# Four graph layers on one core: one return transfer per group of attention, x in memory as it lies on the chip, and layer 0's last outputs inside layer 1's first steps

## The chip, the cores and the metric

The kernel runs on one core of one Trainium2 chip. TensorE (PE) multiplies matrices; VectorE (DVE), ScalarE (ACT) and GpSimd (POOL) work elementwise; SyncE (SP) issues most transfers and POOL issues the rest. Each engine takes its instructions in the order of the program and waits on semaphores for the others. The metric is the device time of one execution in microseconds. Times are medians of several runs; one execution is profiled, and its trace is what the document reads.

## The reference

The input x has shape (128, 64, 256): 128 graphs of 64 nodes with 256 features, that is 8192 tokens. Four layers follow each other, each as x = x + layer(max(layernorm(x), 0)), all in float32:

```
layer 0: h = relu(adj @ (x @ Wg0 + bg0)); h = relu(adj @ (h @ Wg1 + bg1))
         for p in 1..4: cut the nodes into windows of p, run an LSTM over each window,
                        put its last hidden state in the place of the window's last node
layer 1: Xq = H @ W_lin.T; Xv = H @ W_val.T                    (4 heads, 512 edges)
         e = a . leaky_relu(Xq[src] + Xq[dst]) + log(adj[src, dst] + eps)
         attn = softmax of e over the edges with the same src
         Y[src] += attn * Xv[dst]; result Y @ W_out.T
layer 2: agg = A_hat @ x; batchnorm(relu(batchnorm(agg @ W1.T + b1)) @ W2.T + b2)
layer 3: attention of every node over the nodes that adj allows (one head)
```

## The kernel before

The 8192 tokens are cut into NCH = 16 chunks of CHUNK = 512; four chunks make a group (NGR = 4 groups of 2048). A chunk is on the chip as a tile [128, 4, 256]: partition p holds four tokens, tile i holds tokens 128 i to 128 i + 127. Between layers, x is kept in memory in one tensor per chunk, `xa[n]` after layer 0 and `xb[n]` after layer 1, in the order of tokens: 512 rows of 1 KB. The values of layer 1, `xv_mem[n]`, are stored as [128, 4, 256] instead.

Instructions are issued by a framework that orders them by its own priorities; `late(...)` holds an instruction at its place in the program's order. It also inserts the waits between engines and the waits for memory that is used again.

**Layer 0.** Graph convolutions of the 16 chunks run first. `edge_tables()` is a generator, stepped between them, that prepares small tables for layer 1 on DVE, among them `row_of`: for each of the 512 edges (NE = 4 columns of 128) the row of the `field` in which its attention goes. The fields are cleared at the same time by transfers on SP. Then come the LSTMs, for w = 1 to 4 steps and in two halves (groups 0 and 1, groups 2 and 3). PE's products are at L643; the elementwise gates follow in a pipeline, slot by slot, and a gate's tail runs two slots after its products. `group_out(g, c)` (L768) closes a group: for two chunks it transposes the hidden state back (`add_transposed`: four transposes on PE, L167, into one bank; then an add on DVE, L172, to the tile `xres`), and stores `xa[n]` from POOL (L776). The original x for that add is loaded by `fetch_x` (L764) into one of four `xres` buffers. When the last group's LSTM ends, two calls of `group_out` are left, for chunks 12, 14, 13 and 15; they run at the end of layer 0, after the last gate. Chunks 0 and 1 are loaded and normed for layer 1 during the last LSTM (`first_norms1`).

**Layer 1.** It opens with the transposes of chunk 0 (`transpose_features`, L153; copied to `hTs[0]` by ACT, L156) and `project(0)`, `project(1)` (L948). Then `edges(q)` runs for q = 0 to 31, two tiles of 128 tokens each: `gather` (PE L964, copied by ACT L970, leaky ReLU on DVE L971), `project` of the two tiles after next, in even steps the transposes of the next chunk, in odd ones the scaling of the chunk after it, and `score` (L980). `load_x1` (L875) brings a chunk's x from `xa` to one of two buffers. The weights of layer 2 (`w1T` and so on) are loaded on SP ahead of the loads of x.

After each group of eight steps `edge_softmax(g)` is stepped in between later work. It ends by scattering the attention of the group into DRAM: POOL issues eight indirect transfers (L1074), four for each parity par (even and odd graphs lie in the lower and the upper 64 partitions), to `fields1[2 * g + par]`. A field has T * T rows of 64 values, one row for each pair of nodes, and E more rows for edges whose pair has come up already. From the field the attention comes back to the chip as `dense[g]` [128, 64, 64] (L1054): for groups 0 to 2 one transfer of 1 MB for each parity, each as soon as its parity's four scatters have landed; for the last group four of 0.5 MB. `turn_attention(n)` (L1130, half on ACT and half on DVE) puts a chunk's share into `att`.

From step 24 on, `values_of(n)` finishes chunk after chunk: `weigh` (PE L1148: attention times values), `put_out` (PE L1169: times W_out; DVE L1179: add x), `sums` (statistics for layer 2, on DVE and POOL), a store of `xb[n]`. `fetch(n)` loads, two chunks ahead, the values `xv_in` (L1111) and x (`xo`, L1121) on SP. Layers 2 and 3 load x from `xb`.

Of the kernel before, what the change touches and what calls it, by code (L numbers as in the profile page):

```python
# [30 lines left out]
def gnn_stack_kernel(ctx: ExitStack, tc: tile.TileContext, a: dict, out: bass.AP):  # L31
# [21 lines left out]
    xa = [dram.tile([CHUNK, D], F32, tag=f"xa{n}", name=f"xa{n}") for n in range(NCH)]  # L53
    xv_mem = [dram.tile([P, 4, D], F32, tag=f"xv{n}", name=f"xv{n}") for n in range(NCH)]
    xb = [dram.tile([CHUNK, D], F32, tag=f"xb{n}", name=f"xb{n}") for n in range(NCH)]
# [203 lines left out]
    row_of = tabs.tile([P, NE], I32, tag="row_of", name="row_of")  # L259


    FIELD = T * T + E
    NF = 2 * NGR
# [4 lines left out]
    def edge_tables():  # L268
        with ExitStack() as setup:
# [99 lines left out]

            nc.vector.tensor_scalar(earlier, earlier, 0.0, None, ALU.is_equal)  # L370
            nc.vector.tensor_scalar(index, index, float(T * T), None, ALU.add)
# [3 lines left out]
            nc.vector.tensor_copy(row_of, pair)  # L375
# [31 lines left out]

    with ExitStack() as l0:
        w0 = l0.enter_context(tc.tile_pool(name="w0", bufs=1))
# [175 lines left out]
        xres = lpool("xres", 4)  # L585
# [176 lines left out]
        def fetch_x(n):  # L762
            xt = xres.tile([P, 4, D], F32, tag="xres", name="xres")
            nc.sync.dma_start(out=xt, in_=token_tiles(a["x"], n))  # L764
            return xt
# [3 lines left out]
        def group_out(g, c):  # L769

            for u in range(2):
                n = 4 * g + 2 * u + c
                xt = residual.pop(n)
                for ip in range(2):
                    add_transposed(xt, 2 * ip, hTs0[g % 2][:, u], c * CHUNK + ip * 256)
                nc.gpsimd.dma_start(out=token_tiles(xa[n]), in_=xt)  # L776
                if g < 2:
                    m = n + NCH // 2
                    nc.sync.dma_start(
                        out=hTs0[g][:, u, :, c * CHUNK : (c + 1) * CHUNK], in_=hmem[m]  # L780
                    )
# [28 lines left out]
        for slot in range(len(tasks) + 2):  # L810
            new = tasks[slot] if slot < len(tasks) else None
            if new:
                step = steps[new[0]]
                one = step.gate(new[1])
                next(one)
# [11 lines left out]
            if new:  # L827
                next(one)
                flight.append((new, one))
                at, k = new[0], new[2]  # L830
                while outs and outs[0][0] <= slot:
                    group_out(*outs.pop(0)[1:])

                new_half = at + 1 < len(steps) and at and steps[at + 1].w == 1 < step.w
                if k == len(step.gates) - (1 if new_half else 2) and at + 1 < len(steps):
                    steps[at + 1].prepare()
                if step.w == MAX_SKIP and step.t == 2 and k < 2:
                    for u in range(2):
                        n = 4 * step.g + 2 * u + k
                        later.append((slot, "x", n))  # L840
# [7 lines left out]
            if old:  # L848
                (at, q, k), step = old[0], steps[old[0][0]]
                if k == len(step.gates) - 1:  # L850
                    if at + 1 == len(steps) or steps[at + 1].phase != step.phase:
                        phase_over(step.phase)
                    if step.phase == len(phases) - 1 and step.t == 1 and step.g == NGR - 1:

                        t_ = wsp.tile([P, 2, 4, 2, P], F32, tag="wih", name="x_first", bufs=2)
                        flat = t_.rearrange("p k q j m -> p k (q j m)")
                        norms1 = {}
                        for n in range(2):
                            xt = flat[:, n, :].rearrange("p (i d) -> p i d", i=4)
                            nc.sync.dma_start(out=xt, in_=token_tiles(xa[n]))  # L860
                            norms1[n] = Norm(xt)
                        norm_steps = first_norms1(norms1)
                    if step.w == MAX_SKIP and step.t == MAX_SKIP - 1:
                        outs += [(slot + 1, step.g, 0), (slot + 2, step.g, 1)]
        for _ in norm_steps:
            pass
        for _, g, c in outs:
            group_out(g, c)
    psums["banks"] = None
    w12 = ctx.enter_context(tc.tile_pool(name="w12", bufs=1, side="right"))  # L870
    xin1 = l01.enter_context(tc.tile_pool(name="xin1", bufs=2, side="right"))

    def load_x1(n, chunks=xa):
        xt = xin1.tile([P, 4, D], F32, tag="xin1", name="xin1")
        nc.sync.dma_start(out=xt, in_=token_tiles(chunks[n]))  # L875
        return xt


    with ExitStack() as l1:
# [7 lines left out]

        t1 = pool("t1", 2)
        lrp = pool("lrp", 6)
        t3 = pool("t3", 4)  # L890
        w1 = pool("w1", 1)
        vp = pool("vp", 3)
        KEPT = 4
        vk = pool("vk", KEPT)
        yp = pool("yp", 2)
        xo = pool("xo", 4)
        e1 = pool("e1", 1)
        attp = pool("attp", 3)
        attc = pool("attc", 3)
# [4 lines left out]
        nc.sync.dma_start(out=wout, in_=a["W_outT"])  # L904


        w1T = w12.tile([P, 2, 512], F32, tag="w1T", name="w1T")
        nc.sync.dma_start(out=w1T, in_=a["W1T"])
        w2T = w12.tile([P, 4, D], F32, tag="w2T", name="w2T")
        nc.sync.dma_start(out=w2T, in_=a["W2T"])  # L910
        w1S = w12.tile([P, 3, 2, P], F32, tag="w1S", name="w1S")
        w1Q = quarter_sums(w1T.rearrange("p k (q j m) -> p k q j m", q=2, j=2), w1S)
        x_rs = w12.tile([P, NCH, 4], F32, tag="x_rs", name="x_rs")
        x_nm = w12.tile([P, NCH, 4], F32, tag="x_nm", name="x_nm")
        vec = {}
        for name, width in (("b1", 4), ("g1", 4), ("be1", 4), ("b2", 2), ("g2", 2), ("be2", 2)):
            vec[name] = w12.tile([P, width], F32, tag=name, name=name)
            nc.sync.dma_start(out=vec[name], in_=a[name])
        hTs, queries, values, scores, waiting = {}, {}, {}, {}, []
# [20 lines left out]
        def project(it):  # L940

            n, i = it // 4, it % 4
            if i == 0:
                kept = n >= NCH - KEPT
                values[n] = (vk if kept else vp).tile([P, 4, D], F32, tag="xv", name="xv")
# [44 lines left out]
        def edge_softmax(g):  # L990
# [52 lines left out]
            sent = [[], []]  # L1043

            dense[g] = attp.tile([P, T, T], F32, tag="dense", name="dense")

            def bring_back(par, parts=1):
                for k in range(parts):
                    part_back(par, k, parts)

            def part_back(par, k, parts):

                r, s = slice(par * T, (par + 1) * T), slice(k * 32 // parts, (k + 1) * 32 // parts)
                back = nc.gpsimd.dma_start(  # L1054
                    out=dense[g][r, :, :].rearrange("p (o s) r -> p o s r", o=2)[:, :, s, :],
                    in_=fields1[2 * g + par][: T * T, :].rearrange("(t o s) r -> t o s r", t=T, o=2)[
                        :, :, s, :
                    ],
                )
                if g == NGR - 1:  # L1060
                    late(back)
                for ins in sent[par]:
                    tc.add_manual_dep(
                        back.ins,
                        ins.ins.name,
                        mybir.DependencyInfo(mybir.DependencyClass.Sync, mybir.DependencyReason.DATA),
                        reason="rows of the field",
                    )

            if g == NGR - 1:  # L1070
                yield
            for par in range(2):
                for ec in range(NE):
                    ins = nc.gpsimd.indirect_dma_start(  # L1074
                        out=fields1[2 * g + par][:, :],
                        out_offset=bass.IndirectOffsetOnAxis(ap=row_of[:, ec : ec + 1], axis=0),
# [3 lines left out]
                    for earlier in sent[par]:  # L1080
                        tc.declare_no_dep(ins.ins, earlier.ins, reason="different rows")
                    sent[par].append(ins)
                    if g == NGR - 1:
# [7 lines left out]
                        if len(sent[0]) + len(sent[1]) in (3, 6):  # L1091
                            yield
                    elif ec % 2:
                        yield
            if g == NGR - 1:

                for k in range(2):
                    for par in range(2):
                        part_back(par, k, 2)
            else:  # L1100
                bring_back(0)
                yield
                bring_back(1)

        def fetch(n):
# [6 lines left out]
            if n < NCH - 3:  # L1112
                xt = xo.tile([P, 4, D], F32, tag="xo", name="xo")
# [7 lines left out]
            nc.sync.dma_start(out=xt, in_=token_tiles(xa[n]))  # L1121
            fetched[n] = (xv, xt)

        def turn_attention(n):

            g, m = n // 4, n % 4
            att = attc.tile([P, 2, 8, T], F32, tag="att", name="att")
# [55 lines left out]
        def sums(n, xt, keep=False):  # L1183
# [6 lines left out]
            rs, nm = x_rs[:, n, :], x_nm[:, n, :]  # L1190
# [51 lines left out]
        def flush_stores():  # L1242
            while stores:
                m, xt = stores.pop()
                nc.sync.dma_start(out=token_tiles(xb[m]), in_=xt)
# [11 lines left out]
        def edges(q):  # L1257
# [5 lines left out]
            for it in tiles:  # L1263
                if it + 2 < NT:
                    project(it + 2)
            if not odd:
# [20 lines left out]
        hTs[0] = t1.tile([P, 2, CHUNK], F32, tag="hT1", name="hT1")  # L1287
        for ip in range(2):
            transpose_features(norms1[0].h, hTs[0], ip)
# [3 lines left out]
        for q in range(NT // 2):  # L1293
            edges(q)
            last_one = q == NT // 2 - 1
# [10 lines left out]
        def scale_x(n, xt, keep=late):  # L1306

            h2[n] = hpool.tile([P, 4, D], F32, tag="h", name="h")
            for i in range(4):
# [5 lines left out]
                        bias=x_nm[:, n, i : i + 1],  # L1315
                        scale=x_rs[:, n, i : i + 1],
# [17 lines left out]
    l01.close()  # L1334


    with ExitStack() as l2:
# [7 lines left out]
        def load_x2(n):  # L1345
            xt = xin2.tile([P, 4, D], F32, tag="xin2", name="xin2")
            nc.sync.dma_start(out=xt, in_=token_tiles(xb[n]))
# [275 lines left out]
        def fetch(n):  # L1623
            xts[n] = as_tokens(hs[n][1])
            nc.sync.dma_start(out=xts[n], in_=token_tiles(xb[n]))
# [335 lines left out]
```

## Time and profile before

| | us |
|---|---|
| median of 3 runs | 2087.89 |
| the runs | 2086.41, 2092.74, 2087.89 |
| the profiled execution | 2079.25 |
| its span | 2077.5 |

| engine | busy us | share of the span |
|---|---|---|
| PE | 2013.7 | 97% |
| DVE | 1359.9 | 65% |
| ACT | 1180.2 | 57% |
| POOL | 315.7 | 15% |

The granted clock of TensorE is 0.994 on average. 135.06 MB are moved. The span runs from the first to the last instruction of the profiled execution; that execution's own time is 1.75 us longer. The median of the runs without a profile is 8.64 us above the profiled one. A share of busy time is an average over stages: layer 0 fills the span up to about 1285 us, layer 1 from there to about 1690, layers 2 and 3 the rest. "L643" is line 643 of the kernel; a line can be that of a helper that several places call. An arrow such as `xin<-xa` names what is written and what is read, without buffer numbers.

### The profile page before, as it was taken

What the parts mean: (1) busy time and instruction counts of PE and PEld (TensorE: products, weight loads), DVE (VectorE), ACT (ScalarE), POOL (GpSimd) and SP (SyncE); (2) the same over time, 40 slices, a digit from 0 to 9 for tenths busy, and PEclk for the clock granted to TensorE, in tenths of its full rate; (3) what the DMA queues carried; (4) which work ended last, traced back from release to release, by engine and by line L of the source; (5) the groups of instructions that cost most, each with busy time, mean ns of one, the idle gap of its engine ahead of it and who ended that gap; (6) DMA issues with size and microseconds to landing.
All of it is one profiled execution on the core that took longest, in us unless ns stands there. A gap on an engine that the chain in (4) does not pass through costs nothing.

```text
span 2077.5 us, 25503 instructions
## 1 busy us (share of the span) xinstructions
PE 2013.7 (97%) x9444; PEld 1350.0 (65%) x9444; DVE 1359.9 (65%) x2508; ACT 1180.2 (57%) x2226; POOL 315.7 (15%) x422
## 2 busy tenths in 40 slices
PE   8999999999999999999999998999999999999998
PEld 6777478866688845886667886333334765434786
DVE  7664666564665567567446555677777767786776
ACT  4344766554555467566456563666675456592444
POOL 3000010110100021002001001223233420000563
PEclk9999999999999999999999999999999999999999
DMA  8421000100100160001001006213234851022012
GB/s 276 134 96 52 0 21 1 41 0 1 41 1 1 64 220 21 1 1 41 1 0 41 1 1 205 74 51 98 76 92 123 253 185 59 0 71 91 31 62 71
DMA packets 94460, 135.06 MB, mean 65 GB/s; under 512 B 6400, under 2 KB 82048, under 8 KB 92160
## 3 DMA queue, kind: packets, MB, share of 16 engines
q1 hardware_dynamic: 87616, 109.11, 16.0%
q0 software_dynamic: 6112, 24.12, 4.0%
q8 instruction: 74, 1.21, 0.2%
q14 instruction: 50, 0.41, 0.1%
q10 hardware_dynamic: 608, 0.20, 0.0%
HBM read 87.28 MB, written 46.14 MB: 64 GB/s over the span
## 4 chain that ended last, share of the span: by engine, by line
PE 87%; DVE 6%; ACT 3%; DMA 2%; issue 1%; POOL 1%; ACTq 0%; POOLq 0%; DVEq 0%; SPq 0%
PE pa L643 25%; PE bank L50 13%; PE pc L643 13%; PE pb L643 6%; PE pair L964 6%; PE bank L948 5%; PE pa L1396 5%; PE bank L980 3%; PE bank L1169 3%; PE pc L1396 2%; PE pb L1396 1%; PE pair L50 1%; ACT gate L671 1%; PE pair L1148 1%; PE bank L167 1%
## 5 line engine op out<-in xcount | busy, mean ns | idle before, releaser
L643 PE MATMUL pa<-xop,sih 128*128 128x256 f32 (+2 forms) x1056 | 344.3, 418 | 10.1 <-DVE gate L697 6.4
L671 ACT ACTIVATE gate<-gate,bias 128x256 f32<-128x256 f32 (+2 forms) x368 | 247.1, 678 | 173.5 <-DVE gate L687 91.2
L643 PEld LDWEIGHTS pa<-xop,sih 128*128 128x128 f32 x1056 | 198.3, 190 | 86.4 <-issue 22.8
L643 PE MATMUL pc<-xop,wih 128*128 128x256 f32 (+2 forms) x736 | 251.1, 423 | 0.0
L687 DVE TENSOR_TENSOR gate<-pb,gate 128x256 f32<-128x256 f32 (+2 forms) x184 | 87.6, 476 | 225.7 <-PE pb L643 154.1
L643 PE MATMUL pa<-lstm_h,shh 128*128 128x256 f32 (+1 forms) x672 | 212.7, 398 | 0.0
L971 DVE SCALAR_TENSOR_TENSOR lr<-lr 128x1024 f32<-128x1024 f32 x128 | 150.5, 1218 | 55.6 <-ACT lr L970 55.6
L643 PEld LDWEIGHTS pc<-xop,wih 128*128 128x128 f32 x736 | 139.8, 190 | 51.2 <-issue 23.0
L702 DVE TENSOR_TENSOR gate<-pc,gate 128x256 f32<-128x256 f32 (+2 forms) x184 | 87.6, 476 | 119.7 <-PE pc L643 119.4
L970 ACT COPY lr<-pair 128x1024 f32<-128x1024 f32 x128 | 123.1, 1014 | 45.1 <-PE pair L964 45.1
L643 PEld LDWEIGHTS pa<-lstm_h,shh 128*128 128x128 f32 x672 | 127.7, 190 | 30.2
L643 PE MATMUL pc<-lstm_h,whh 128*128 128x256 f32 (+1 forms) x448 | 141.8, 398 | 0.0
L686 ACT COPY gate<-pa 128x256 f32<-128x256 f32 (+2 forms) x184 | 76.0, 413 | 96.7 <-PE pa L643 96.4
L964 PE MATMUL pair<-sd_hot,xq 64*128 64x512 f32 x512 | 127.6, 616 | 2.4 <-ACT lr L970 2.3
L948 PE MATMUL bank<-wlv,hT 128*128 128x512 f32 x256 | 118.1, 604 | 0.2 <-ACT hT L156 0.2
L697 DVE TENSOR_TENSOR gate<-pa,gate 128x256 f32<-128x256 f32 (+2 forms) x184 | 87.5, 475 | 44.0 <-PE pa L643 43.4
L691 ACT COPY gate<-pa 128x256 f32<-128x256 f32 (+2 forms) x184 | 75.4, 410 | 59.0 <-PE pa L643 57.7
L671 ACT ACTIVATE gate<-pa,bias 128x256 f32<-128x256 f32 (+2 forms) x184 | 94.0, 511 | 26.1 <-PE pa L643 24.4
L434 POOL TENSOR_TENSOR sih<-wih 128x512 f32<-128x512 f32 x8 | 11.8, 1474 | 624.8 <-DMA wih<-in_WihT 295.9
L643 PE MATMUL pa<-xop,wih 128*128 128x256 f32 (+1 forms) x320 | 101.4, 398 | 2.7 <-ACT xop L624 2.7
L643 PE MATMUL pb<-xop,wih 128*128 128x256 f32 (+1 forms) x320 | 100.3, 398 | 1.6 <-DVE gate L687 1.6
L643 PEld LDWEIGHTS pc<-lstm_h,whh 128*128 128x128 f32 x448 | 85.1, 190 | 20.1
(338 smaller groups left out, 3814.8 us busy)
## 6 DMA issues: line engine op xcount, KB each, us to landing
field<-sd_hot SPq DMA_DIRECT2D x8, 1152.0 KB, 11.4
wih<-in_WihT SPq DMA_DIRECT2D x8, 1024.0 KB, 5.0
xres<-in_x SPq DMA_DIRECT2D x16, 512.0 KB, 4.5
xa<-xres POOLq DMA_DIRECT2D x16, 512.0 KB, 5.3
xin<-xb SPq DMA_DIRECT2D x16, 512.0 KB, 3.9
h<-xb SPq DMA_DIRECT2D x16, 512.0 KB, 3.9
xin<-in_x SPq DMA_DIRECT2D x15, 512.0 KB, 5.5
out_x<-h SPq DMA_DIRECT2D x15, 512.0 KB, 2.9
```

Of the source, the lines that this page charges most:

```text
L50: nc.tensor.matmul(o, lhsT, rhs, start=start, stop=stop)
L643: ins = nc.tensor.matmul(p[:, : self.N], weights[kind, self.phase](k, q), x[k], start=first_ and kind == "ih", stop=kind == "hh" or not se ...
L671: nc.scalar.activation(out, in_, AF.Tanh if q == 2 else AF.Sigmoid, bias=bias[:, self.w - 1, 2 * q + j : 2 * q + j + 1],)
L686: nc.scalar.copy(blk[0, 0], pa[:, :N])
L687: nc.vector.tensor_tensor(blk[0, 0], pb[:, :N], blk[0, 0], ALU.add)
L697: nc.vector.tensor_tensor(blk[1, 1], pa[:, :N], blk[1, 1], ALU.add)
L702: nc.vector.tensor_tensor(blk[1, 0], pc[:, :N], blk[1, 0], ALU.add)
L948: ins = nc.tensor.matmul(p, hTs[n][:, k, i * P : (i + 1) * P], wlv[:, k, :], start=k == 0, stop=k == 1)
L964: ins = nc.tensor.matmul(p[:, par, :], queries[it][r, c * P : (c + 1) * P], sd_hot[r, :], start=True, stop=True)
L970: nc.scalar.copy(lr, p)
L971: nc.vector.scalar_tensor_tensor(lr, lr, 0.2, lr, ALU.mult, ALU.max)
L1396: ins = nc.tensor.matmul(p, lhs[k], x[k], start=first_, stop=last_one, skip_group_check=True)
```

## The change

It has three parts.

**One return per group.** The fields of both parities of a group become one DRAM tensor: FIELD is doubled and NF, their number, is halved. `row_of` gets a second set of rows for the second parity, computed by three more small DVE operations in `edge_tables`. The eight scatters of a group write to the one field, and one transfer of 128 rows of 16 KB brings the 2 MB back, on POOL, after all eight. This holds for the last group, too.

**x in memory as on the chip.** `xa[n]` and `xb[n]` are [128, 4, 256] in DRAM, so that each partition's four tokens are one run of 4 KB. All stores and loads of them follow.

**Layer 0's last outputs in layer 1's first steps.** The two calls of `group_out` that are left go to a list, `last_outs`, and `edges(0)` and `edges(1)` do one each, after their projections. The transposes of chunk 0 move into layer 0, to the slot after the last gate's products have been begun; PE has them before the last ten products, and their result lies in a gate's buffer (`first_hT`). The pools `w0` and `xres` live on to the end of `edges(1)`; then `layer2_weights()` loads layer 2's weights, and the pools `vk`, `xo` and `attc` are opened. The last four loads of `xres` come after the loads of layer 1's weights. On SP the order at the seam is then: layer 1's weights, four `xres`, x of chunks 2 and 3, layer 2's weights, x of chunk 4, four `xo`. The pools of layer 1 are declared in another order.

```diff
-    xa = [dram.tile([CHUNK, D], F32, tag=f"xa{n}", name=f"xa{n}") for n in range(NCH)]
+    xa = [dram.tile([P, 4, D], F32, tag=f"xa{n}", name=f"xa{n}") for n in range(NCH)]
...
-    FIELD = T * T + E
-    NF = 2 * NGR
+    FIELD = 2 * (T * T + E)
+    NF = NGR
...
-            nc.vector.tensor_scalar(index, index, float(T * T), None, ALU.add)
+            nc.vector.tensor_scalar(index, index, float(2 * T * T), None, ALU.add)
...
-            nc.vector.tensor_copy(row_of, pair)
+            nc.vector.tensor_copy(row_of[:, 0, :], pair)
+            nc.vector.tensor_scalar(earlier, earlier, float(T * T - E), float(E), ALU.mult, ALU.add)
+            nc.vector.tensor_tensor(pair, pair, earlier, ALU.add)
+            nc.vector.tensor_copy(row_of[:, 1, :], pair)
...
+    l0out = ExitStack()
+    w0 = l0out.enter_context(tc.tile_pool(name="w0", bufs=1, side="right"))
...
-                nc.gpsimd.dma_start(out=token_tiles(xa[n]), in_=xt)
+                nc.gpsimd.dma_start(out=xa[n], in_=xt)
...
+            if slot == len(tasks):
+                for _ in norm_steps:
+                    pass
+                first_hT = gp.tile([P, 4 * NMAX], F32, tag="gate", name="hT1_first")
+                first_hT = first_hT[:, : 2 * CHUNK].rearrange("p (c t) -> p c t", c=2)
+                for ip in range(2):
+                    transpose_features(norms1[0].h, first_hT, ip, late)
...
-                if step.w == MAX_SKIP and step.t == 2 and k < 2:
+                if step.w == MAX_SKIP and step.t == 2 and k < 2 and step.g < NGR - 1:
...
-        for _ in norm_steps:
-            pass
-        for _, g, c in outs:
-            group_out(g, c)
+        last_outs = [(g, c) for _, g, c in outs]
...
+        for g, c in last_outs:
+            for u in range(2):
+                n = 4 * g + 2 * u + c
+                residual[n] = fetch_x(n)
...
-                        out=fields1[2 * g + par][:, :],
-                        out_offset=bass.IndirectOffsetOnAxis(ap=row_of[:, ec : ec + 1], axis=0),
+                        out=fields1[g][:, :],
+                        out_offset=bass.IndirectOffsetOnAxis(ap=row_of[:, par, ec : ec + 1], axis=0),
...
+            back = nc.gpsimd.dma_start(
+                out=dense[g].rearrange("p s r -> p (s r)"),
+                in_=fields1[g][: 2 * T * T, :].rearrange("(p s) r -> p (s r)", p=P),
+            )
             if g == NGR - 1:
-                for k in range(2):
-                    for par in range(2):
-                        part_back(par, k, 2)
-            else:
-                bring_back(0)
-                yield
-                bring_back(1)
+                late(back)
...
-            nc.sync.dma_start(out=xt, in_=token_tiles(xa[n]))
+            nc.sync.dma_start(out=xt, in_=xa[n])
...
-                nc.sync.dma_start(out=token_tiles(xb[m]), in_=xt)
+                nc.sync.dma_start(out=xb[m], in_=xt)
...
+            if last_outs:
+                group_out(*last_outs.pop(0))
             if not odd:
...
-        hTs[0] = t1.tile([P, 2, CHUNK], F32, tag="hT1", name="hT1")
-        for ip in range(2):
-            transpose_features(norms1[0].h, hTs[0], ip)
+        hTs[0] = first_hT
         sums1(2, (0, 1))
         for it in range(2):
             project(it)
         for q in range(NT // 2):
             edges(q)
+            if q == 1:
+                l0out.close()
+                layer2_weights()
+                for name, bufs in (("vk", KEPT), ("xo", 4), ("attc", 3)):
+                    later_pools[name] = pool(name, bufs)
```

## The prediction

> **What bounds the kernel now.** I read four views, in this order. First the page: which engine is busy, and which ends the chain of waits.
>
> ```profile
> span 2077.5 us, 25503 instructions
> ...
> PE 2013.7 (97%) x9444; PEld 1350.0 (65%) x9444; DVE 1359.9 (65%) x2508; ACT 1180.2 (57%) x2226; POOL 315.7 (15%) x422
> ...
> PE 87%; DVE 6%; ACT 3%; DMA 2%; issue 1%; POOL 1%; ACTq 0%; POOLq 0%; DVEq 0%; SPq 0%
> ```
>
> TensorE is the bound almost everywhere. A change that takes no matmul away can win only where PE stands idle, so I looked for idle PE in the two places that the change touches. The first is the seam between layer 0 and layer 1, in the timeline of PE (start, duration, instructions; in brackets the idle time before and what ended it):
>
> ```profile
> 1272.17 0.59 PE L643 MATMUL pc<-lstm_h,whh 128*128 128x256 f32 x2
> 1277.02 6.51 PE L167 MATMUL bank<-ident,hT 128*128 128x128 f32 x32 [4.26 <-DVE hT L737]
> 1283.37 1.04 PE L153 MATMUL bank<-ident,h 128*128 128x128 f32 x8
> 1284.64 3.70 PE L948 MATMUL bank<-wlv,hT 128*128 128x512 f32 x8 [0.24 <-ACT hT L156]
> ...
> 1309.06 2.04 PE L964 MATMUL pair<-sd_hot,xq 64*128 64x512 f32 x8 [2.03 <-ACT lr L970]
> ```
>
> The last LSTM product ends at 1272.76. PE then waits 4.26 us for the last gates and spends 6.51 us on the 32 output transposes, although at 0.13 us each (L153: 1.04 for 8) they are 4.16 us of work: the eight adds of 0.69 us on DVE pace them. Only at 1284.64 does layer 1 start. A second loss follows: project(6,7) starts 11.50 us after project(4,5) (1311.03 against 1299.53), where later odd steps take 9.32 (1321.22 to 1330.54). The chain of waits and SP's timeline name its cause: chunk 2's load sat behind w1T, which could be issued only at 1291.70.
>
> ```profile
> 1295.46 4.06 DMA xin<-xa
> ```
>
> The second place is the end of layer 1, PE's timeline again, and below it the table by stretch (PE, PEld, DVE, ACT, POOL busy; granted clock; DMA share; GB/s):
>
> ```profile
> 1646.54 3.72 PE L1169 MATMUL bank<-wout,yT 128*128 128x256 f32 x16
> 1654.41 1.99 PE L1148 MATMUL pair<-att,xv_in 64*64 64x64 f32 x64 [4.15 <-DMA xv_in<-xv]
> 1656.33 5.11 PE L1169 MATMUL bank<-wout,yT 128*128 128x256 f32 x16
> ...
> 1663.82 1.04 PE L1148 MATMUL pair<-att,xv 64*64 64x64 f32 x56 [2.11 <-DVE att L1130]
> ```
>
> ```profile
> 1515.00:1525.00 10.00, 10.00 (x46) 3.53 (x44) 4.62 (x5) 6.64 (x12) 3.85 (x6) 1.00 0.99 210
> 1650.00:1655.00 5.00, 0.85 (x23) 0.62 (x25) 1.67 (x10) 0.00 (x0) 4.51 (x10) 0.73 1.02 193
> 1655.00:1660.00 5.00, 5.00 (x66) 4.24 (x59) 1.48 (x10) 1.01 (x1) 4.10 (x12) 0.58 1.08 239
> ```
>
> Here the DMA engines are full. PE waits 4.15 us for chunk 11's values, then 2.11 for the last group's attention, and between them runs at a low clock: 5.11 us for what took 3.72.
>
> **What the Trainium skill says.** "DMA: Bandwidth & Descriptors", Rules for kernel authors: two transfers to disjoint partition halves serialize, and one over 128 partitions is to be used. The trace agrees as to rate: two halves of 1 MB move together at 210 GB/s (stretch 1515 to 1525). The same page, Queues, rings and completion order: an engine serves its queues in turn, a packet at a time. The trace agrees only in that a queue of long rows takes more of the time: in 1653 to 1657 the queue of the field's return had 97% of it, the loads 7%. Same page, Why small descriptors are slow: the overhead per packet matters at 256 bytes; for rows of 1 KB against 4 KB that promises little. The trace agrees: xv_in (4 KB rows) lands in 3.2 to 4.3 us in quiet stretches, xin (1 KB rows) in 3.8 to 3.9. "TensorE: Matmul & The Clock Gate", HAM oscillation: waits for a DMA let the clock fall to half. The trace agrees: 0.58 after the 4.15 us.
>
> **The change part by part.**
>
> *Layer 0's last outputs in layer 1's first steps.* Removed at the seam: between the last product and project(0,1) lie 11.88 us (1272.76 to 1284.64). In the new order the eight transposes of chunk 0 (1.04) stand before the last ten products, and I add 0.4 for their bank, as layer 0 shares two. The last product then ends at 1274.2 and project(0,1) follows at once, its hT copied long before: 10.4 us earlier. The last gate's chain (ACT, DVE, until about 1278) is covered by project and gather, 3.70 + 1.99 + 3.70 us. Returned: 16 transposes each in the first two steps, 2.08 us of PE, and 0.5 for banks, since four adds of 0.69 on DVE are 2.8: project(4,5) moves from 1299.53 to 1291.7 (−7.8), and the second step costs 2.6 again. Removed there: the 2.18 us (11.50 − 9.32) of chunk 2's lateness, because its load is now ahead of w1T on SP. What it queues behind: wlv and wout, which are issued much earlier in the program, and the four last xres loads, the fourth of which waits for group 2's last xa store. Those loads went out until 1272.42 before, and nothing in that chain moves. xin(2) also waits for PE's work on the memory that it takes; I put it at 1274.4, landing (4.06) at 1278.5, needed at about 1282.4. DMAs: four xa stores on POOL come 4 to 15 us later, but their first readers are layer 1's chunks 12 to 15. POOL's quarter sums of w1T come behind them, needed in layer 2. Sum: −10.4 + 2.6 + 2.6 − 2.2 = **−7.4 us**.
>
> *One return per group.* For groups 0 to 2 the return has slack (group 2 landed by 1613, needed 1615.6): 0; without that cover it would cost 1:1. For the last group four 0.5 MB pieces, issued from 1640.13 to 1646.6, landed by 1660.1. The single one must wait on POOL for all eight scatters, 1645.4; what is queued behind it, small steps of x's norm and the sums of w2T, stood behind the last pieces too. 2 MB took 12.0 us from first issue to last landing in group 0 and 13.8 in group 2, among other traffic: 1657.4 to 1659.2; I take 1658.9, −1.2. On the way chunk 11's values (issued 1643.77) get the engines alone for some 3 us and come before PE wants them, so weigh(11) and put_out(11) run at about 1650 to 1655 at full speed. But PE then idles 6 to 8 us before weigh(12), which starts cold: 0.83 on it (1.99 − 1.16) and 1.39 on its put_out. What is late next is DVE's half of att(12), behind the adds of chunk 10, whose xo was issued at 1649.76 and landed 11.12 us later:
>
> ```profile
> 1649.76 11.12 DMA xo<-xa
> ```
>
> The return starves it as the pieces did, until about 1660. Weigh(12) thus starts some 1.9 us earlier at best, 1 later at worst, and pays 2.2 cold: **+0.3**, bounds −3.5 (loads and return both in time, no cold clock) and +4.3 (chunk 11's values land only after the return, at 1661: 6.6 us later than now, of which 2.3 are hidden because weigh(12) then needs no wait of its own). The two DVE adds of put_out(9), now behind POOL's small steps, are hidden: done near 1656, their bank wanted at 1664.8.
>
> *x as on the chip.* The loads and stores in quiet stretches are hidden behind PE. One is on the chain, h<-xb at 1917.13 (3.29): 4 KB rows take perhaps 0.3 off. Bounds 0 and −1: **−0.3**. The conv stage's clearing of four larger fields (same bytes, back to back on SP) makes chunk 8's x land at about 61 us instead of 52, needed at 75, and its tables come four steps sooner on a DVE that is 100% busy from 35 to 50: 0, bounds ±2.
>
> Sum: −7.4 + 0.3 − 0.3 = −7.4. The profiled execution, 2079.25 (span 2077.5), becomes 2071.9. The median of the runs, 2087.89, lies 8.6 above it, so I set the forecast there: 2087.9 − 7.4 = **2080.5 us**. No change within 0.3% (6.3 us, about what a measurement of this kernel can tell) means 2081.6 to 2094.2.
>
> **The rivals.**
>
> *B, the end of layer 1 gains too.* With chunk 11's values early and xo(10) landing before 1657, the weigh of chunk 12 comes at about 1660 without a cold clock: −3 more, **2077.5**. For it: the pieces' slowness lies in mixing with other loads. Against it: the stretch above, where alone they reach no more than 210 GB/s.
>
> *C, the return starves the loads.* Rows of 16 KB instead of 4 KB take an even larger share, and chunk 11's values land at 1661: +4.3, **2084.8**, no change. For it: 97% against 7%. Against it: these values were issued 1.6 us before the return can be.
>
> *D, slower.* Chunk 2's x is late again, in the program's new order: xin(2) stands on SP behind the four xres loads, and on DVE its statistics stand ahead of the copies of xv, of the adds of the outputs and of lr, so that banks are not freed and PE stops. Each us of landing beyond 1282.4 is a us. At 1289.8 the gain is gone, at 1296.1 it is slower by 0.3%; before, it landed at 1299.5. That landing would give +9.7, **2097.6**. For it: the stall of 2.03 us above is of this kind. Against it: nothing ahead of it on SP waits for layer 1, unlike w1T.
>
> **How the numbers follow.** A 55%, its own range 2077.5 to 2083.5 (conv stage ±2, bank waits ±1, a median of three that spans 6 us); B 18%; C 17%; D 10%. Eight in ten: 2073.5 (B with a gain in the conv stage) to 2088.5 (C with a loss there, or a mild D). Faster by over 0.3%: B and 0.7 of A, 0.57. Slower: most of D, a little of C, 0.10. The rest, 0.33.
>
> **What would show it.** Right: project(0,1) starts within 2 us of the last LSTM product; two groups of 16 L167 with waits under 1 us; no idle of 2 us before project(6,7); project(6,7) 7 to 8 us earlier by the span; the last return issued near 1645.4 − 7.4 and landing 12 to 14 us later; PE idle over 5 us before weigh(12), with a low clock after. Wrong: L87 or L172 on DVE waiting for xin<-xa past 1282, PE idle before weigh(11) as now, or a conv stage that ends more than 2 us apart from before.

## The result

The changed kernel takes 2074.22 us (median of 4 runs, 2071.39 to 2075.99), the kernel before beside it 2088.51. The ratio is 0.9929, with an interval of 0.9912 to 0.9946: 11 to 18 us less. Two later sets gave 0.9944 (0.9929 to 0.9960; 2068.39 us against 2080.16) and 0.9934 (0.9921 to 0.9946; 2067.75 against 2080.40). The forecast was 2080.5 us, 7.4 us less than before. The time lies in the forecast's range, 2073.5 to 2088.5, close to its lower end, and the sign is right; the gain is nearer 13 us than 7.4.

The page of the changed kernel shows the same engines, as busy as before:

```profile
span 2073.3 us, 25490 instructions
...
PE 2014.8 (97%) x9444; PEld 1353.1 (65%) x9444; DVE 1363.6 (66%) x2511; ACT 1183.8 (57%) x2226; POOL 306.0 (15%) x416
```

The seam between layers 0 and 1, in the timeline of PE (start, duration, instructions, idle time before and its releaser):

```profile
1272.38 0.59 PE L651 MATMUL pc<-lstm_h,whh 128*128 128x256 f32 x2
1272.81 3.60 PE L970 MATMUL bank<-wlv,hT_first 128*128 128x512 f32 x8
...
1281.79 1.91 PE L167 MATMUL bank<-ident,hT 128*128 128x128 f32 x16
...
1301.04 3.70 PE L970 MATMUL bank<-wlv,hT 128*128 128x512 f32 x8
```

Project(0,1) follows the last LSTM product with no idle time, and the output transposes lie inside layer 1's steps with hardly a wait (1.91 us here, 2.39 for the second group at 1293.03). Project(6,7) starts at 1301.04, where it was 1311.03. At the end of layer 1 the same view shows:

```profile
1581.29 0.34 PE L1150 MATMUL pair<-att,xv_in 64*64 64x64 f32 x4 [0.38 <-issue]
...
1647.09 1.16 PE L1150 MATMUL pair<-att,xv_in 64*64 64x64 f32 x64
...
1656.67 1.77 PE L1150 MATMUL pair<-att,xv 64*64 64x64 f32 x56 [4.49 <-DVE att L1132]
1658.38 5.72 PE L1171 MATMUL bank<-wout,yT 128*128 128x256 f32 x16
```

Chunk 11 (1647.09) no longer waits for its values. PE waits before weigh(12) instead, 4.49 us, and the low clock follows, as forecast. What the trace of before had not shown are the gaps marked "issue" inside one weigh.

Between the two traces shown the span falls by 4.2 us only, while the medians differ by 14.3. The profiled execution of before is one without such gaps, 8.6 us under its own median; the changed kernel's has them. Before took 2086.45 us in a set of runs whose traces all have gaps, 2080.16 and 2080.40 in two sets without. Each of these three sets ran on another chip, so the gaps may belong to the chip or to the session and not to chance; the first traces of before and after have no chip on record. So I cut every trace into four stages by starts in PE's timeline, and compare only traces that are alike in these gaps:

| kernel | start to first LSTM product | to project(6,7) | to first product of layer 2 | to the end | gaps |
|---|---|---|---|---|---|
| before, first trace | 194.04 | 1116.99 | 375.95 | 390.52 | no |
| before, second trace | 193.11 | 1118.16 | 382.69 | 395.34 | yes |
| seam alone | 193.64 | 1109.08 | 381.46 | 392.12 | yes |
| return alone | 192.69 | 1117.24 | 379.89 | 390.58 | yes |
| layout alone | 192.58 | 1114.87 | 382.36 | 390.49 | yes |
| after, first trace | 192.88 | 1108.16 | 380.57 | 391.69 | yes |
| after, second | 192.77 | 1108.86 | 373.53 | 390.84 | no |
| after, third | 193.15 | 1108.28 | 373.06 | 395.01 | no |
| before, 16 buffers | 193.17 | 1118.34 | 375.93 | 390.66 | no |
| after, 16 buffers | 193.09 | 1108.40 | 371.34 | 395.17 | no |
| after, no scatters in group 2 | 194.23 | 1109.01 | 373.16 | 390.70 | no |
| after, return in pieces | 192.67 | 1107.65 | 380.06 | 391.82 | no |
| after, att(12) first | 192.67 | 1108.99 | 368.66 | 391.08 | no |
| before, x loaded first | 192.76 | 1122.08 | 376.18 | 391.78 | no |

The last stage, layers 2 and 3, varies by 5 us from trace to trace in both kernels. The stages before it are steady: the seam takes 9.4 us less (1117.8, the mean of the three traces of before that have no change there, to 1108.4 in the three of after), the rest of layer 1 2.4 to 2.9 less without gaps, and 2.1 less with them.

### The profile page after: what moved, and what is told of

Read it like the earlier page. It is cut to its first block, busy times and chain, and to the rows that moved or that the text cites. A ratio compares the mean times of both kernels' runs of the same rounds, so it can differ in the third digit from the quotient of the medians.

```text
span 2073.3 us, 25490 instructions
## 1 busy us (share of the span) xinstructions
PE 2014.8 (97%) x9444; PEld 1353.1 (65%) x9444; DVE 1363.6 (66%) x2511; ACT 1183.8 (57%) x2226; POOL 306.0 (15%) x416
## 5 line engine op out<-in xcount | busy, mean ns | idle before, releaser
L970 PE MATMUL bank<-wlv,hT 128*128 128x512 f32 x240 | 110.7, 604 | 0.0
```

The costliest lines, as they stand in the source:

```text
L970: ins = nc.tensor.matmul(p, hTs[n][:, k, i * P : (i + 1) * P], wlv[:, k, :], start=k == 0, stop=k == 1)
```

## The experiments

**The parts one by one.** The kernel before again, and the kernel before with one part of the change each. The seam alone is everything on `last_outs`, `first_hT`, the pools and `layer2_weights`; the return alone is `fields1`, `row_of` and the one `back`; the layout alone is:

```diff
-    xa = [dram.tile([CHUNK, D], F32, tag=f"xa{n}", name=f"xa{n}") for n in range(NCH)]
+    xa = [dram.tile([P, 4, D], F32, tag=f"xa{n}", name=f"xa{n}") for n in range(NCH)]
...
-                nc.gpsimd.dma_start(out=token_tiles(xa[n]), in_=xt)
+                nc.gpsimd.dma_start(out=xa[n], in_=xt)
```

> The kernel before, unchanged, for a second trace: its runs lie 7 to 13 us above its one profiled execution, those of the changed kernel do not. Theory (the end of layer 1 is where an execution differs from the next): the seam takes 11.9 us from the last LSTM product to project(0,1) again, within 0.3, and if this execution is a usual one (span near 2086) PE's waits in the last 50 us of layer 1 come to some 13 to 15 us, against 6.3 in the first trace. Rival (a slower clock, or stalls all over): the waits at the end of layer 1 stay near 6 and the 8 us are spread over the layers. Time: ratio 1.000.

> The kernel before with layer 0's last outputs in layer 1's first steps alone; fields, return and layout as before. Theory (the seam makes the gain): project(0,1) within 0.5 us of the last LSTM product, project(6,7) about 10 us earlier than before by the LSTM's start, two groups of 16 output transposes of 1.9 to 2.4 us; time 8 to 10 us below before, ratio 0.9955 +- 0.001. Rival (return and layout make half of it, since the medians differ by 14 and the seam is worth 7.4 to 10): ratio about 0.9965 and only_return at or below 0.997. Second rival (the end of layer 1 gives it back, since all there comes sooner into the same transfers): ratio over 0.998.

> The kernel before with one field and one return per group alone. Theory: 0 to +3 us, ratio 0.9995 to 1.0015: PE no longer waits for chunk 11's values, but for weigh(12), which DVE's queue holds up behind statistics that wait for GpSimd, and it pays the low clock all the same. Rival (the pieces were what made the end of layer 1 slow in most executions): 4 to 8 us faster, ratio 0.996 to 0.998. Second rival (a return of long rows starves the loads): chunk 11's values land after 1660, 4 us slower, ratio 1.002.

> The kernel before with xa and xb in memory as on the chip alone. Theory: h<-xb at the start of layer 3 lands in 2.8 to 3.1 us instead of 3.29, all else is hidden: -0.3 us, ratio 0.9995 to 1.0. Rival (a quarter of the packets leaves the DMA engines free for the transfers at the end of layer 1): chunk 11's values land before 1651, PE's waits for transfers there drop by 3 us or more, ratio 0.998 or below.

| kernel | median us | ratio to before (2086.45) | interval |
|---|---|---|---|
| before again | 2086.73 | 1.0001 | 0.9993 to 1.0009 |
| seam alone | 2077.87 | 0.9958 | 0.9945 to 0.9971 |
| return alone | 2084.64 | 0.9993 | 0.9983 to 1.0002 |
| layout alone | 2084.30 | 0.9989 | 0.9980 to 0.9997 |

The seam makes 8.8 us of the gain. The product of the three ratios, 0.9940, agrees with the whole within the intervals. These are 3.5 to 5.4 us wide, too wide to show whether the parts overlap by an us or two. The second trace of before answers where its usual executions lose time against the first trace:

```profile
1591.51 0.34 PE L1148 MATMUL pair<-att,xv_in 64*64 64x64 f32 x5 [0.38 <-issue]
...
1662.37 1.99 PE L1148 MATMUL pair<-att,xv_in 64*64 64x64 f32 x64 [4.96 <-DMA xv_in<-xv]
```

Its waits at the end of layer 1 are as in the first trace (4.96 and 1.01 us, against 4.15 and 2.11), so my expectation of 13 to 15 us there fell. The 6.7 us more of that stage come with the gaps in weigh, and 4.8 more lie in layers 2 and 3.

The return alone, PE:

```profile
1655.97 1.16 PE L1132 MATMUL pair<-att,xv_in 64*64 64x64 f32 x64
...
1665.05 1.43 PE L1132 MATMUL pair<-att,xv 64*64 64x64 f32 x56 [3.29 <-DVE att L1114]
```

Chunk 11 runs on time and full speed; PE waits 3.29 us at chunk 12 and 0.62 just before. The stage is 2.8 us shorter than in the second trace of before. The time's interval, −3.5 to +0.4 us, allows the 0 to +3 that was expected only at its upper edge, and no change at all; the gain is read from the one trace.

The layout alone gained about 2 us, where I had expected 0.3. Its gain is not where it was expected: PE's wait at the start of layer 3 is 3.82 or 3.83 us in every trace of either kernel. It is at the seam of the old order:

```profile
1305.48 2.04 PE L964 MATMUL pair<-sd_hot,xq 64*128 64x512 f32 x8 [0.61 <-ACT lr L970]
```

That wait was 2.03 us before, and project(6,7) comes 10.05 us after project(4,5), not 11.50. In the whole change this is no gain of its own, because the seam removes that wait anyway (11.55 with 2.39 us of transposes in it, and no wait of 0.3 us or more).

**Which queue holds the end of layer 1.** The changed kernel again:

> The changed kernel, unchanged, for a second trace beside the next runs. Theory: -12 to -14 us against before, ratio 0.993 to 0.9945; PE's wait before weigh(12) 4 to 5 us and the low clock after it again, with DVE's aggregates waiting for GpSimd's x_nm some 5 us in all just before; stalls of PE in weigh that the profile marks as issue, at group 2's scatters and at the last group's. Rival (the tail of the first trace was an accident): PE's wait before weigh(12) differs by over 2 us or has another releaser.

In this second trace of it, DVE (above; BATCH_NORM_AGGREGATE makes the mean and variance of a chunk) and PE (below):

```profile
1641.83 0.38 DVE L1191 BATCH_NORM_AGGREGATE ln_mv<-ln_st 128x2 f32<-128x6 f32 x4 [2.58 <-POOL x_nm L1197]
...
1650.48 0.58 DVE L1132 COPY att<-dense 128x512 f32<-128x512 f32 x1
```

```profile
1646.51 0.34 PE L1150 MATMUL pair<-att,xv 64*64 64x64 f32 x8 [0.90 <-ACT att L1132]
1651.11 1.77 PE L1150 MATMUL pair<-att,xv 64*64 64x64 f32 x56 [4.26 <-DVE att L1132]
```

The attention is back by 1645.40, when ACT copies its half. DVE copies its half at 1650.48: it has lost 5.9 us (1.69, 2.58 and 1.64) waiting for GpSimd to read older means and variances, of which there are four buffers, and is behind with the adds. There were no gaps marked issue in this set, on either kernel. The next two kernels give these values 16 buffers:

```diff
-            mv = stat.tile([P, 4, 2], F32, tag="ln_mv", name="ln_mv")
+            mv = stat.tile([P, 4, 2], F32, tag="x_mv", name="x_mv", bufs=16)
```

> The changed kernel with 16 buffers instead of 4 for the means and variances of layer 2's statistics, so that DVE's aggregates don't wait until GpSimd has read older ones. Theory (DVE's queue holds up att(12), the return has long landed): DVE copies att(12) as soon as the return lands, about 10 us after its issue; PE waits 1 to 2 us instead of 4.5 before weigh(12) and stays at full clock; 3 to 6 us faster than the changed kernel, ratio to before 0.990 to 0.992. Rival (the return is what is late): DVE then waits for dense, PE's wait stays over 4 us, time within 1 us of the changed kernel.

> The kernel before with the same 16 buffers. Theory: there PE waits first for chunk 11's values and then for att(12), whose pieces land last; so the buffers bring little, 0 to -2 us, ratio 0.999 to 1.0. Rival (the statistics' wait was a brake before as well, through stores and loads that follow the adds): -3 us or more, ratio below 0.9985.

With them in the changed kernel (2069.22 us, ratio 0.9944, 0.9929 to 0.9960; 2068.39 for the changed kernel beside it) the time is the same: the expected 3 to 6 us didn't come. The stage is 2.2 us shorter in the one trace, less than the 6 us that the interval spans, so the medians can't confirm it. Now DVE does wait for the return (3.05 us, until 1645.51), then copies att(13), does the two adds of chunk 10, and only then att(12) at 1648.35; PE waits 1.15 + 2.04 us and the clock still falls. By this trace each account held half: the wait for GpSimd was 2.2 us of it, the return's landing and the rest of DVE's order the remainder. In the kernel before the buffers do nothing (2080.60 us, 1.0001, 0.9992 to 1.0009), as expected: there the attention lands at 1660.6, after everything else.

**DVE's order.** On top of the 16 buffers, att(12) stands ahead of the adds in the program:

```diff
             flush_stores()
+            if n + 1 == LAST:
+                turn_attention(LAST)
             flush_values()
-
-            if n + 1 == LAST:
-                turn_attention(LAST)
```

> The changed kernel with the 16 buffers for means and variances, and att(12) put ahead of the adds of chunk 10 in the program. Theory (after the buffers, what is left of PE's wait is DVE's order: att(13) and two adds before att(12)): weigh(12) runs whole as soon as the attention has landed; PE waits 1 to 1.5 us in all there, not 3.2, and no low clock after; from project(6,7) to layer 2 about 368 us without stalls (371.3 with the buffers alone, 373.5 in the changed kernel); 4 to 6 us faster than the changed kernel, ratio to before 0.991 to 0.9925. Rival (PE's idle time comes back at the next wait for a transfer): the wait moves to chunk 12 or 13's x, and the time is within 2 us of the changed kernel.

> The changed kernel again, as the measure for the runs beside it: ratio to before 0.993 to 0.995; from project(6,7) to the first product of layer 2 it takes 373.5 us if PE has no stalls marked issue there, 380 to 381 if it has.

```profile
1647.99 1.16 PE L1150 MATMUL pair<-att,xv 64*64 64x64 f32 x64 [2.38 <-ACT att L1132]
1649.09 3.72 PE L1171 MATMUL bank<-wout,yT 128*128 128x256 f32 x16
```

One wait of 2.38 us is left, for the return itself, and the clock stays up (3.72, not 4.83 to 5.72). The stage takes 368.66 us, 4.4 less than in the changed kernel beside it. The time is 2064.02 us, ratio 0.9919 (0.9905 to 0.9932), against 2067.75 and 0.9934 (0.9921 to 0.9946): 3.7 us less, a little under the 4 to 6 expected. The intervals against before overlap, but the slowest of its six runs (2066.23) is below the fastest of the six beside it (2066.82). It is the fastest kernel of the study. The order without the 16 buffers was not run.

**One transfer or pieces.** In the changed kernel, the last return is cut into four of 0.5 MB again, all after the eight scatters:

```diff
-            back = nc.gpsimd.dma_start(
-                out=dense[g].rearrange("p s r -> p (s r)"),
-                in_=fields1[g][: 2 * T * T, :].rearrange("(p s) r -> p (s r)", p=P),
-            )
+            for k in range(2):
+                for par in range(2):
+                    r, s = slice(par * T, (par + 1) * T), slice(k * 16, (k + 1) * 16)
+                    part_back(
+                        dense[g][r, :, :].rearrange("p (o s) r -> p o s r", o=2)[:, :, s, :],
...
```

> The changed kernel, with the last group's return cut in four pieces of 0.5 MB again, all after the eight scatters, the fields as changed. Theory (one transfer of 16 KB rows is what lands sooner: about 10 us after its issue, where the pieces took 14.5): the attention is there 3 to 5 us later than in the changed kernel, PE waits that much longer before weigh(12), less what DVE's queue took anyway: 1 to 3 us slower than the changed kernel, chunk 11's values late again or not. Rival (4 KB rows of x and the order of loads made the end of layer 1 quicker, not the return): attention within 1 us of the changed kernel, time the same.

Issue on POOL and first copy on ACT, from the timeline:

```profile
1633.36 2.44 POOL L1094 DMA_DIRECT2D dense<-field  x4 [4.19 <-DMA field<-attn,row_of]
...
1651.82 1.07 ACT L1146 COPY att<-dense 128x512 f32<-128x512 f32 x1 [10.05 <-DMA dense<-field]
```

The four pieces need 18.5 us from the first issue to use; the one transfer needed 10.4 to 12.2 in the traces without gaps. PE waits 8.65 us for it. The stage is 7.0 us longer than with one, the time 6.1 us (2073.85 us, ratio 0.9964, 0.9950 to 0.9977). This is more than expected: the rival, that the return doesn't matter, is out. It agrees with the Trainium skill, "DMA: Bandwidth & Descriptors", Rules for kernel authors, that one transfer over 128 partitions is to be used.

The pieces differ from the one transfer in three ways: their number, their 64 partitions and their rows of 4 KB instead of 16. Group 1's return tells something of the rows. There the kernel before sends two halves of 64 partitions and the return alone sends one transfer of 128, both in rows of 16 KB. The same stretch of either trace, before above, with the DMA share and GB/s at the end:

```profile
1516.00:1522.00 6.00, 6.00 (x20) 2.32 (x18) 2.82 (x4) 3.65 (x7) 3.56 (x6) 1.00 1.03 218
```

```profile
1516.00:1522.00 6.00, 6.00 (x22) 2.28 (x24) 2.78 (x3) 4.04 (x9) 2.54 (x4) 1.00 1.01 322
```

The DMA engines are busy all the time in both, yet one transfer moves 322 GB/s and two halves 218. The page says that halves gain nothing; here they cost a third of the rate. So long rows alone don't make the rate, and a full DMA share is not the highest rate. Whether it is the 64 partitions or the two transfers at once was not taken apart.

**Scatters and gaps.** Group 2's scatters are left out, the rest stays:

> The changed kernel without the eight scatters of group 2 (its attention is left out of the result; the return stays). Theory (PE's stalls marked issue in the weigh under these scatters come with them: both want the DMA engines, PE for its instructions): that weigh runs 1.2 us without a gap and its put_out at 3.7; the gaps under the last group's scatters remain; 3 to 5 us faster than the changed kernel. Rival (the stalls belong to that place in PE's instructions): the gaps at group 2's weigh remain, time within 1 us.

The time is 2068.21 us (0.9945, 0.9929 to 0.9961), as for the changed kernel beside it (2068.39). But that set of runs had no gaps marked issue at all, with or without the scatters, so the run doesn't tell what makes them. It shows that group 2's scatters cost PE nothing when there are none.

**Chunk 2's load.** In the kernel before, the loads of chunks 2 and 3 stand ahead of w1T:

```diff
+        coming1 = {n: load_x1(n) for n in (2, 3)}
         w1T = w12.tile([P, 2, 512], F32, tag="w1T", name="w1T")
...
-        coming1 = {n: load_x1(n) for n in (2, 3)}
         hTs[0] = t1.tile([P, 2, CHUNK], F32, tag="hT1", name="hT1")
```

> The kernel before with the loads of chunks 2 and 3 placed ahead of layer 2's weights on SP, nothing else. Theory (chunk 2's lateness costs the 2.2 us between project(4,5) and project(6,7)): that step falls from 11.5 to 9.3 us, ratio to before 0.999. Rival (the wait is for something else, such as layer 0's outputs on DVE): the step stays at 11.4 or more, time the same.

SP and PE:

```profile
1293.13 0.91 SPq L875 DMA_DIRECT2D xin<-xa  x2
1294.09 0.49 SPq L908 DMA_DIRECT2D w1T<-in_W1T  x1
```

```profile
1312.09 2.82 PE L964 MATMUL pair<-sd_hot,xq 64*128 64x512 f32 x8 [2.02 <-ACT lr L970]
```

It brought nothing (2080.89 us, 1.0002, 0.9993 to 1.0011). Two views say why. The first is SP's longest wait, in before (above) and with x first (below):

```profile
SPq L908 <- DMA xa<-xres: 13.1, 2, 11.8
```

```profile
SPq L875 <- DMA xa<-xres: 13.6, 2, 12.0
```

Whichever load stands first waits 12 us until the stores of layer 0's last outputs have landed. So chunk 2's load goes out at 1293.13, 7.6 us after project(0,1) (1285.55), where it was 10.8: sooner, but not soon. The second view is the chain that ended last, with x first:

```profile
1294.09 6.09 DMA w1T<-in_W1T
...
1301.15 1.66 POOL w1S L136
...
1306.74 0.58 POOL ln_rs L99
...
1309.57 1.57 ACT h L109 x3
```

Chunk 2 has landed when DVE takes its statistics at 1297.55, but GpSimd can't norm it yet: the quarter sums of w1T (L136) stand ahead in its queue, and w1T itself, now behind x, lands only at 1300.18, so that the sums end at 1306.1 (1298.4 in the first trace of before). In the first trace of before the chain goes through chunk 2's load instead (1295.46, 4.06 us). The edit thus moved the wait from one load to the other. It does not show that chunk 2's lateness was harmless. In this trace project(4,5) also comes 17.05 us after project(0,1) (14.88 before) and project(6,7) 12.24 after that, because the clock falls after the wait (2.82 us for a gather that takes 1.99).

## Why the prediction was right, and where its sums were off

*The seam* was read rightly, and is the larger part of the gain: −9.4 us by the stages, −8.8 by the run of that part alone, against −7.4 in the sum. By its terms (means of the same traces): the last product comes 1.3 us later (forecast 1.44). Project(0,1) follows it 12.0 to 12.5 us sooner (forecast 11.88). The step that was mis-sized is "16 transposes each in the first two steps, 2.08 us of PE, and 0.5 for banks": the first group costs 1.8 us (16.68 from project(0,1) to project(4,5), not 14.88), the second 2.2 (11.55 to project(6,7), not the 9.32 of a later odd step), and the banks next to nothing, so that 1.2 us of the returned 5.2 never came. The chunk-2 term, −2.2, has about the right size (2.2 to 2.9 in the traces of before), but only half of its cause. Chunk 2's load does stand behind w1T on SP, 3.8 us of issues later (1291.70 to 1295.46). But w1T itself waits 11.8 us for the stores of layer 0's last outputs to land; these are issued until 1284.56 in the first trace. With x first the same wait holds x, and w1T then holds GpSimd. The prediction didn't name these stores. That the loads wait because they reuse these outputs' memory is my reading; no run took away the memory alone. In the changed kernel xin(2) goes out at 1272.58, before the stores.

*The return* has the wrong sign: forecast +0.3 (bounds −3.5 and +4.3), measured −2.4 to −2.9 in the stage without gaps. Its first half came as told: chunk 11 on time, PE idle before weigh(12) (4.5 to 5.2 us, forecast 6 to 8), low clock after. Two sizes failed. "2 MB took 12.0 us from first issue to last landing in group 0 and 13.8 in group 2 … I take 1658.9", which is 13.5 after the issue, was 10.4 to 12.2. These groups were measured as two halves, which moved 210 to 218 GB/s in group 1; one transfer of 128 partitions moved 322 there in the return alone, so the halves' time was the wrong measure for it. (The 13.8 also counts from the second half's issue, 1600.42; from the first, 1598.66, it is 15.5.) "Here the DMA engines are full" was true of their time and not of their rate. And "pays 2.2 cold" was 0.9 to 1.8: from weigh(12) to layer 2 it takes 24.05 to 24.94 us, against 23.16 before. Weigh(12) starts 3.3 to 4.0 us sooner after project(6,7) in the second and third traces, where I had allowed 1.9 at best. The note that statistics on DVE behind GpSimd's small steps "are hidden" was wrong as well: the adds of chunks 9 and 10 stand behind them, and att(12) behind these.

*The layout* was put at −0.3 on layer 3's first load; nothing came there. Loads of h from xb do land sooner, in 3.2 us instead of 3.9 (medians), but PE's wait stays. Alone the layout is worth about 2 us, of which 1.5 lie at the seam's old wait and vanish in the whole change.

*The rivals.* B, a gain at the end of layer 1 too, came in part: its gain of about 3 us did, but not without the low clock. C, loads starved by the long return, did not come: weigh(11) starts on time in all traces with one return. D did not come: DVE takes chunk 2's statistics at 1280.90 without a wait.

*That the time lay in the range was partly luck.* The range's low end stood for a gain in the conv stage, and none came (192.8 to 193.2 us against 193.1 to 194.0 to the first LSTM product). The time fell there because the seam gave 2 us more than its sum and the end of layer 1 gave 2.4 to 2.9 where a loss of 0.3 was forecast.

*The 8.6 us between the first trace and its median* were carried over as a constant. That was good enough only because within each set of runs both kernels have the gaps or neither; as a difference of two traces, the change would have been read as 4 us.

## What to carry to other kernels

Work that ends one stage behind a wait can be put into the first steps of the next, if those keep the engine busy while the wait runs out; the price is its bare matmul time. When a transfer on the way to the bound engine gets faster, look at the in-order queue of the engine that hands its data over: here the next 4 us lay in DVE's order and in four small buffers, changed together. When moving a load ahead doesn't help, ask what it displaced and who waits for that. And a trace can lack a stall that the runs timed beside it have, so cut traces into stages and compare stages, not spans.

## What the runs showed of the hardware that I had not expected

PE stalled inside a weigh with no releaser in the trace: 0.36 to 0.41 us every 4 to 6 matmuls around group 2's scatters, and once in each of two weighs (0.46 to 0.48 and 0.37 to 0.39 us) under the last group's. In the first trace of after this stretch took 4.9 us more from that weigh to the next gather (9.65 us against 4.74 in the first trace of before), and the whole stage some 7 us more. It appeared in the first trace of after and in every trace of the first set of runs, in none of the two later sets, in both kernels alike and at nearly the same matmuls. Its cause stays open, a difference between chips among the candidates.

Before weigh(12), a PE wait of 2.38 us left the clock up, and waits of 3.2 to 5.2 us in all brought it down (1.31 to 1.77 us for 56 matmuls that otherwise take 1.04). That is no threshold: with x loaded first, a wait of 2.02 us brought it down as well, while 2.03 us in the first trace of before did not. Four transfers of half the partitions took 18.5 us from issue to use for the 2 MB that one transfer brought in 10.4 to 12.2. And the DMA engines, busy all the time in both cases, moved 218 GB/s with two halves and 322 with one transfer, in rows of the same length.
